# Layer 1's values by seven half-width products, sums of pixels on GpSimd, pixels read a pair of chunks at a time

## The chip, the cores and the metric

The kernel runs on one core of a Trainium2 chip. The time is that of one execution of the whole program on the device, in microseconds (us); a kernel is run several times and the median is given. One further execution is recorded by the hardware profiler, and every duration below comes from that record. The engines are called PE (TensorE matmuls), PEld (TensorE's weight loads), DVE (VectorE), ACT (ScalarE), POOL (GpSimd) and SP (SyncE, which here only issues DMAs).

## The reference

Two layers on an image tensor of 2 images, 512 channels and 64 x 64 pixels, all in fp32. Each layer normalizes its input in groups of channels and adds its result to it.

```
x = x + L0(group_norm(x))     # deformable convolution: depthwise 3x3, offsets, masks, bilinear samples
x = x + L1(group_norm(x))     # attention over all 4096 pixels of an image:

px = pixels x channels                      # 4096 x 512 for each image
q, k = tanh(px @ Wq.T), tanh(px @ Wk.T)     # 64 channels each
v = px @ Wv.T
attn = softmax(sum_p q * k * align_w)
content = (px + attn @ v) @ Wfc.T + bfc
out = relu(batch_norm(content))             # statistics over both images
```

The change is in layer 1. The kernel folds the output matrix into the values, so that it makes `v = px @ (Wv.T @ Wfc.T)` once for each image and applies it to the probabilities.

## The kernel before

Layer 0 takes up about the first 1273 us of the recorded execution. The change leaves it alone. Layer 1 then runs once for each of the two images (the loop at L1237), and its instructions stand on each engine's queue exactly in the order of the source (`tc.manual_schedule`). An engine that waits holds up everything behind it on its queue; a DMA waits on the queue of the engine that issues it.

A *chunk* is 512 pixels with all 512 channels, a tile of 128 partitions x 4 channel blocks x 512 pixels (1 MB). An image has eight chunks, taken as four *pairs* `i`. Three stages follow each other in an image.

**Values stage** (L1240 to L1261). For each pair, `pk` (L1245) computes keys and queries of both chunks on PE and `tanh` (L1249) puts them into `kq`. Then four calls of `values(i, x1, x2, t)` (L1197) each take 128 pixels of both chunks of the pair. The matmul at L1204 has pixels as the stationary operand and the folded weights `wc` (512 channels wide) as the moving one. It fills one PSUM bank for each chunk; a matmul of the program appears as two instructions in the trace. From these two banks ScalarE and VectorE make seven planes of 256 channels, the tile `v`: four blocks or differences of blocks of the values, in the form in which the later product needs them, and SP stores the tile to DRAM (`wv`, 0.9 MB). Between calls, ScalarE normalizes the chunks of the next pair (`normalize`, L1134). All chunks of an image are loaded far ahead into `xs` from the pool `cp` (eight buffers); for image 1 they are issued on ScalarE's queue. In the third pair of image 0 `output_weights` (L1215) loads the matrix `wfcT` and makes the planes `w7` from it. In the last pair `produce(0, 0)` and `produce(0, 1)` stand between the calls.

**Attention** (L1265 to L1317). For each of eight query chunks `qb` and each of 16 steps `kp`: `produce(qb, kp + 2)` computes scores (`pS`, L1172), their exponentials `e` (L1176) and four sums on VectorE; `load_values` (L1227) reads six of the seven planes of step `kp + 2` from DRAM (0.8 MB) into a ring of four buffers; six products of 256 columns go into six PSUM banks `acc` (L1309, 24 instructions). Two more steps multiply the pixels of the chunk itself (`xq`, L1288, 1 MB) by `w7`. So the product of attention and values is made of seven block products in place of eight already.

**Seventh product and finish** (L1339 to L1387). The seventh product `p7` (L1347, 72 instructions) reads the seventh planes, loaded one at a time by `load_seventh` (L1232, 0.13 MB, six buffers): six beside the last accumulation steps, ten within `p7` as buffers come free. In the last query chunk of an image these ten go into two tiles of the values ring (L1296). Within the last `p7` of image 0 the chunks and `wc` of image 1 are loaded and its first pair is normalized. Eight PSUM banks are used: `A0` to `A5` through `bank(i, ...)`, and two as one tile with the tag `st` for scores. Names ending in `_d` are in DRAM.

At the end, batch norm needs all of both images. The residuals `xr` (L1337) and the stored chunks `r` (L1403) are loaded, scaled, added and written out (L1426).

Of the kernel before, what the change touches and what calls it, by code (L numbers as in the profile page):

```python
# [9 lines left out]
F32 = mybir.dt.float32  # L10
I32 = mybir.dt.int32
AF = mybir.ActivationFunctionType
# [5 lines left out]
P = 128  # L18
NB = 2
C = 512  # L20
# [550 lines left out]
def window_path(ctx: ExitStack, tc: tile.TileContext, t_in: dict, out: bass.AP, far: bass.AP, sums: bass.AP):  # L571
# [516 lines left out]
    with ExitStack() as l1, tc.manual_schedule():  # L1088
# [8 lines left out]
        with ExitStack() as at, ExitStack() as inner:  # L1097
# [3 lines left out]
            vw = inner.enter_context(tc.tile_pool(name="w1v", bufs=3, side="right"))  # L1101
            ps = at.enter_context(tc.tile_pool(name="w1ps", bufs=1, space=PSUM))
# [25 lines left out]

            def value_output():
                t = wk.tile([P, KB, C], F32, tag="x", name="wc", bufs=1)  # L1130
                nc.sync.dma_start(t, wc_d)
                return t
# [7 lines left out]
            xs = [chunk(0, 0), chunk(0, 1)]  # L1140
            wc = value_output()
            xs += [chunk(0, ch) for ch in range(2, NCH)]
# [9 lines left out]
            normalize(xs[0], *norms[0])  # L1152
            normalize(xs[1], *norms[0])
# [43 lines left out]
            def values(i, x1, x2, t):  # L1197

                cols = slice(t * P, (t + 1) * P)
                pv = []  # L1200
                for h, x in enumerate((x1, x2)):
                    p = bank(2 * (t % 2) + h, "pv")
                    for kb in range(KB):
                        nc.tensor.matmul(p, x[:, kb, cols], wc[:, kb, :], start=(kb == 0), stop=(kb == KB - 1))  # L1204
                    pv.append(p)
                v = vw.tile([P, 7, HC], F32, name="v", bufs=4)
                nc.scalar.copy(v[:, 0, :], pv[0][:, :HC])
                nc.vector.tensor_sub(v[:, 6, :], v[:, 0, :], pv[0][:, HC:])
                nc.scalar.copy(v[:, 1:6:4, :], pv[1].rearrange("p (a c) -> p a c", a=2))
                nc.vector.tensor_add(v[:, 3, :], v[:, 5, :], pv[0][:, HC:])  # L1210
                nc.vector.tensor_sub(v[:, 2, :], v[:, 3, :], v[:, 0, :])
                nc.vector.tensor_sub(v[:, 4, :], v[:, 1, :], v[:, 2, :])
                nc.sync.dma_start(v_d[n][4 * i + t], v)

            def output_weights():  # L1215

                wfc = load_w("wfcT", C, cp, tag="c")
                wf4 = wfc.rearrange("p (h r) (i c) -> p h r i c", h=2, i=2)
                nc.scalar.copy(w7[:, :, 0, :], wf4[:, 0, :, 0, :])
                nc.scalar.copy(w7[:, :, 1, :], wf4[:, 1, :, 0, :])  # L1220
                nc.scalar.copy(w7[:, :, 5, :], wf4[:, 1, :, 1, :])
                nc.vector.tensor_sub(w7[:, :, 6, :], wf4[:, 0, :, 0, :], wf4[:, 0, :, 1, :])
                nc.vector.tensor_add(w7[:, :, 3, :], wf4[:, 0, :, 1, :], wf4[:, 1, :, 1, :])
# [3 lines left out]
            def load_values(n, kp):  # L1227
                v = vw.tile([P, 7, HC], F32, name="v", bufs=4)
                nc.sync.dma_start(v[:, :6, :], v_d[n][kp][:, :6, :])
                return v  # L1230

            def load_seventh(n, kp):  # L1232
                v = wk.tile([P, HC], F32, name="v7", bufs=6)
# [3 lines left out]
            for n in range(NB):  # L1237
                sc, bi = norms[n]
                ready = []
                for i in range(NCH // 2):  # L1240
                    for h in range(2):
                        ch = 2 * i + h
                        pk = bank(4 + h, "pk")
                        for kb in range(KB):
                            nc.tensor.matmul(  # L1245
                                pk, wkq[:, h, kb].rearrange("p h d -> p (h d)"), xs[ch][:, kb, :],
                                start=(kb == 0), stop=(kb == KB - 1),
                            )
                        nc.scalar.activation(kq[:, ch, :], pk, AF.Tanh)  # L1249
                    if i == 0:  # L1250
                        queries(0)
                    for t in range(4):
                        values(i, xs[2 * i], xs[2 * i + 1], t)
# [223 lines left out]
```

## Time and profile before

| what | us |
|---|---|
| median of three runs (3728.24 to 3731.88) | 3728.55 |
| the profiled execution, its own time | 3727.62 |
| its span, first to last instruction | 3725.8 |
| PE busy / DVE busy / ACT busy / POOL busy | 3443.0 / 2249.3 / 1290.7 / 220.5 |
| products of values, L1204, 512 instructions, PE busy | 222.4 |
| attention products, L1309, 256 columns, with `e` / with `tt` | 768.2 / 748.2 |
| seventh product, L1347, with values | 231.1 |
| values stage of image 0, first product to last | 1290.3 to 1425.1 |
| values stage of image 1, first product to last | 2468.4 to 2601.5 |

The mean granted TensorE clock over the span was 0.968 of full speed. "Busy" is the time in which at least one instruction of the kind runs; the mean length of a matmul in a group row is longer than the distance from one to the next, because matmuls are pipelined, so the pace is read from runs of them in the chain of waits.

### The profile page before, as it was taken

The numbers are of one execution on the slowest core, as the hardware profiler recorded it, in microseconds if no ns is written. First come the engines' busy times: TensorE is split into PE (matmuls) and PEld (weight loads), VectorE is DVE, ScalarE is ACT, GpSimd is POOL, SyncE is SP. The second block draws the span as 40 slices with busy tenths as digits, with TensorE's granted clock in tenths as the row PEclk, the third lists the DMA queues.
The fourth block names the chain that finished last, engine by engine and source line by source line (L and its number), as shares of the span: only waits on it lengthen the run. The fifth ranks groups of instructions, "written<-read, shape, count | busy, mean of one in ns | idle before, by whom it ended". The sixth has DMA issues, their size and how long they took to land.

```text
span 3725.8 us, 37930 instructions
## 1 busy us (share of the span) xinstructions
PE 3443.0 (92%) x14735; PEld 2359.8 (63%) x14735; DVE 2249.3 (60%) x3402; ACT 1290.7 (35%) x1659; POOL 220.5 (6%) x162
## 2 busy tenths in 40 slices
PE   4589989999998899999999999999999999999990
PEld 2255555555555446777777777764777777777770
DVE  6899989999996324545554554432455455545544
ACT  1466767777776332111111111122111121111115
POOL 2111112112111000000000000000000000000000
PEclk9789999999999899999999999999999999999995
DMA  6234432433432434334334433443433343343349
GB/s 238 62 98 128 133 123 82 126 121 94 127 96 99 163 120 162 130 109 153 128 115 138 138 131 106 157 171 120 161 120 118 108 144 113 111 135 120 124 150 394
DMA packets 179629, 499.96 MB, mean 134 GB/s; under 512 B 22096, under 2 KB 63824, under 8 KB 169968
## 3 DMA queue, kind: packets, MB, share of 16 engines
q1 hardware_dynamic: 176528, 476.48, 38.2%
q10 hardware_dynamic: 2880, 20.97, 1.4%
q8 instruction: 117, 1.92, 0.2%
q14 instruction: 72, 0.59, 0.0%
q0 software_dynamic: 32, 0.00, 0.0%
HBM read 406.09 MB, written 91.29 MB: 133 GB/s over the span
## 4 chain that ended last, share of the span: by engine, by line
PE 60%; DMA 1%; DVE 0%; ACT 0%; SPq 0%; issue 0%; ACTq 0%
PE acc L1309 41%; PE pS L1172 7%; PE p L1347 7%; PE pv L1204 4%; PE pk L1245 1%; DMA out<-ct 1%; PE pr L1273 0%; DMA v<-wv 0%; DMA r<-wx 0%; ACT ct L1421 0%; DVE r L1425 0%; SPq L1403 0%; ACT r L1421 0%; DVE ct L1425 0%; ACT e L1176 0%
## 5 line engine op out<-in xcount | busy, mean ns | idle before, releaser
L1309 PE MATMUL acc<-e,v 128*128 128x256 f32 x3072 | 768.2, 386 | 2.1 <-DMA v<-wv 2.1
L1309 PE MATMUL acc<-tt,v 128*128 128x256 f32 x3072 | 748.2, 380 | 0.0
L1176 ACT ACTIVATE e<-pS 128x1024 f32<-128x1024 f32 x256 | 262.4, 1025 | 1360.7 <-PE pS L1172 1319.1
L1309 PEld LDWEIGHTS acc<-e,v 128*128 128x128 f32 x3072 | 566.5, 190 | 235.4 <-issue 163.8
L1309 PEld LDWEIGHTS acc<-tt,v 128*128 128x128 f32 x3072 | 582.4, 190 | 90.7 <-issue 10.6
L1179 DVE TENSOR_TENSOR t<-e 128x256 f32<-128x256 f32 x256 | 108.9, 425 | 764.7 <-ACT e L1176 764.7
L786 DVE SCALAR_TENSOR_TENSOR conv<-xn,L_conv_dw_w_sb,conv 128x504 f32<-128x504 f32 (+1 forms) x512 | 400.1, 795 | 18.4 <-ACT conv L781 4.2
L1189 DVE TENSOR_TENSOR tot<-tot,e 128x512 f32<-128x512 f32 x480 | 330.2, 688 | 8.3
L947 PEld LDWEIGHTS pa<-bt,patch 96*128 96x128 f32 x2048 | 252.2, 197 | 62.9 <-issue 38.5
L1172 PE MATMUL pS<-q,kq 64*128 64x512 f32 x1024 | 289.0, 641 | 0.0
L947 PE MATMUL pa<-bt,patch 96*128 96x128 f32 x2048 | 256.2, 282 | 9.3 <-ACT dT L958 5.8
L933 ACT COPY bt<-pb 96x1024 f32<-96x1024 f32 x124 | 234.1, 2001 | 57.1 <-PE pb L928 57.1
L967 PE MATMUL py<-dT,L_conv_out_w_sb 128*128 128x512 f32 x512 | 240.0, 614 | 0.0
L756 PE MATMUL pq<-L_conv_in_w_sb,xn 128*128 128x512 f32 x512 | 236.8, 606 | 2.3 <-ACT xn L746 2.3
L1347 PE MATMUL p<-t,v 128*128 128x256 f32 x1024 | 231.1, 382 | 0.0
L1204 PE MATMUL pv<-wc,xt 128*128 128x512 f32 x512 | 222.4, 593 | 1.4 <-DVE v L1210 1.4
L1347 PEld LDWEIGHTS p<-t,v 128*128 128x128 f32 x1024 | 192.2, 190 | 46.2 <-issue 21.2
L958 ACT COPY dT<-pa 32x256 f32<-32x256 f32 x496 | 180.0, 363 | 111.4 <-PE pa L947 102.1
L840 PE MATMUL po<-om_w_pg,feat 128*128 128x432 f32 x512 | 203.5, 542 | 0.0
L967 PEld LDWEIGHTS py<-dT,L_conv_out_w_sb 128*128 128x128 f32 x512 | 100.4, 200 | 121.5 <-issue 116.7
L1204 PEld LDWEIGHTS pv<-wc,xt 128*128 128x128 f32 x512 | 96.9, 190 | 125.3 <-issue 121.7
L756 PEld LDWEIGHTS pq<-L_conv_in_w_sb,xn 128*128 128x128 f32 x512 | 94.5, 195 | 107.5 <-issue 94.1
(174 smaller groups left out, 3310.6 us busy)
## 6 DMA issues: line engine op xcount, KB each, us to landing
v<-wv SPq DMA_DIRECT2D x256, 768.0 KB
patch<-xt SPq DMA_DIRECT2D x256, 192.0 KB
v<-wv SPq DMA_DIRECT2D x256, 128.0 KB
wv<-v SPq DMA_DIRECT2D x32, 896.0 KB
xt<-xj SPq DMA_DIRECT2D x128, 128.0 KB
res<-in_x SPq DMA_DIRECT2D x64, 256.0 KB
wx<-res SPq DMA_DIRECT2D x64, 256.0 KB
xq<-wx SPq DMA_DIRECT2D x16, 1024.0 KB
```

The costliest lines, as they stand in the source:

```text
L756: nc.tensor.matmul(pq, xn[:, kb, 1 + 2 * t : 3 + 2 * t, :].rearrange("p r c -> p (r c)"), in_w[:, kb, :], start=(kb == 0), stop=(kb == KB ...
L786: nc.vector.scalar_tensor_tensor(dst, src, wt, dst, ALU.mult, ALU.add)
L840: nc.tensor.matmul(po[:, : 3 * GP], f[:, kb, t * P : (t + 1) * P], om_w[:, kb].rearrange("p a k g -> p (a k g)"), start=(kb == 0), stop=(k ...
L933: copy(bt[:SN].rearrange("s g q d -> s d (g q)")[:, d0 : d0 + 4, :], pb[:SN])
L947: nc.tensor.matmul(pa[:, p], xp[:SN, p, cb * P : (cb + 1) * P], bt[:SN, 4 * cb : 4 * cb + 4, PX * s + p, :], start=True, stop=True,)
L967: nc.tensor.matmul(py, out_w[:, kb, cb * P : (cb + 1) * P], dT[:, kb, :], start=(kb == 0), stop=(kb == KB - 1))
L1172: nc.tensor.matmul(pS[:, h, :], kq[r, 2 * (kp // 4) + h, c0 : c0 + P], qs[qb][r, :], start=True, stop=True)
L1176: nc.scalar.activation(e.rearrange("p a q -> p (a q)"), pS.rearrange("p h q -> p (h q)"), AF.Exp)
L1189: nc.vector.tensor_add(tots[qb], tots[qb], e2[:, h, :])
L1204: nc.tensor.matmul(p, x[:, kb, cols], wc[:, kb, :], start=(kb == 0), stop=(kb == KB - 1))
L1309: nc.tensor.matmul(acc[j][:, cb * HQ : (cb + 1) * HQ], v[:, j, cb * P : (cb + 1) * P], ops[j], start=(kp + cb == 0), stop=(kp + cb == NPAI ...
L1347: nc.tensor.matmul(p7[:, cb * HQ : (cb + 1) * HQ], v7[:, cb * P : (cb + 1) * P], t3, start=(k + cb == 0), stop=(k + cb == NPAIR + 2),)
```

## The change

The values of a pair of chunks are a product of matrices of 2 x 2 blocks: two chunks by two halves of the input channels, times two halves of the input channels by two halves of the output channels. The kernel before makes all eight block products. The changed one makes seven, of sums and differences of blocks (`sa`, `sb` of pixels, `wcs` of weights), each of 256 columns and two matmuls deep. Eleven VectorE operations and one ScalarE copy put the seven results together into the same seven planes. The sums of the next pair's pixels are made by GpSimd after its second chunk is normalized; those of image 0's first pair by VectorE. Sums take up buffers of `cp`, so pixels are loaded one pair ahead and not all at once. The values ring becomes a pool of its own with three buffers, the output weights are loaded at the start into two of them, the first two values loads of an image stand on ScalarE's queue after the last call, and seventh planes get 13 buffers.

```diff
+            vv = inner.enter_context(tc.tile_pool(name="w1vv", bufs=3, side="right"))
...
+            def load_pixels(n, i):
+                pair = [chunk(n, 2 * i + h) for h in range(2)]
+                return pair, [cp.tile([P, 2, 2, CH], F32, tag="c", name=name) for name in ("xsa", "xsb")]
+
+            def sum_pixels(engine, pair, sums):
+                (a1, a2), (sa, sb) = [x.rearrange("p (j r) q -> p j r q", j=2) for x in pair], sums
+                engine.tensor_add(sa[:, 0], a2[:, 0], a2[:, 1])
+                engine.tensor_sub(sa[:, 1], sa[:, 0], a1[:, 0])
+                engine.tensor_sub(sb[:, 0], a1[:, 0], a2[:, 0])
+                engine.tensor_sub(sb[:, 1], a1[:, 1], sa[:, 1])
...
+            def sum_value_output(wc):
+                t = wk.tile([P, 2, 4, HC], F32, tag="tx", name="wcs", bufs=1)
+                b = wc.rearrange("p (j r) (l c) -> p j r l c", j=2, l=2)
+                nc.vector.tensor_sub(t[:, :, 0, :], b[:, 0, :, 1, :], b[:, 0, :, 0, :])
+                nc.vector.tensor_sub(t[:, :, 1, :], b[:, 1, :, 1, :], t[:, :, 0, :])
+                nc.vector.tensor_sub(t[:, :, 2, :], b[:, 1, :, 1, :], b[:, 0, :, 1, :])
+                nc.vector.tensor_sub(t[:, :, 3, :], t[:, :, 1, :], b[:, 1, :, 0, :])
+                return t
...
-            xs = [chunk(0, 0), chunk(0, 1)]
+            pixels = {0: load_pixels(0, 0)}
             wc = value_output()
-            xs += [chunk(0, ch) for ch in range(2, NCH)]
+            pixels[1] = load_pixels(0, 1)
...
-            normalize(xs[0], *norms[0])
-            normalize(xs[1], *norms[0])
+            for x in pixels[0][0]:
+                normalize(x, *norms[0])
+            sum_pixels(nc.vector, *pixels[0])
+            wcs = sum_value_output(wc)
...
-            def values(i, x1, x2, t):
+            def values(n, i, t):
                 cols = slice(t * P, (t + 1) * P)
-                pv = []
-                for h, x in enumerate((x1, x2)):
-                    p = bank(2 * (t % 2) + h, "pv")
-                    for kb in range(KB):
-                        nc.tensor.matmul(p, x[:, kb, cols], wc[:, kb, :], start=(kb == 0), stop=(kb == KB - 1))
-                    pv.append(p)
-                v = vw.tile([P, 7, HC], F32, name="v", bufs=4)
-                nc.scalar.copy(v[:, 0, :], pv[0][:, :HC])
-                nc.vector.tensor_sub(v[:, 6, :], v[:, 0, :], pv[0][:, HC:])
-                nc.scalar.copy(v[:, 1:6:4, :], pv[1].rearrange("p (a c) -> p a c", a=2))
-                nc.vector.tensor_add(v[:, 3, :], v[:, 5, :], pv[0][:, HC:])
+                (x1, x2), (sa, sb) = pixels[i]
+                products = (
+                    (x1[:, 0:2], wc[:, 0:2, :HC]), (x1[:, 2:4], wc[:, 2:4, :HC]), (sa[:, 1], wcs[:, :, 1, :]),
+                    (sa[:, 0], wcs[:, :, 0, :]), (sb[:, 1], wc[:, 2:4, HC:]), (sb[:, 0], wcs[:, :, 2, :]),
+                    (x2[:, 2:4], wcs[:, :, 3, :]),
+                )
+                p = []
+                for j, (a, b) in enumerate(products):
+                    if j % 2 == 0:
+                        pv = bank((4 * t + j // 2) % 6, "pv")
+                    p.append(pv[:, (j % 2) * HC : (j % 2 + 1) * HC])
+                    for r in range(2):
+                        nc.tensor.matmul(p[j], a[:, r, cols], b[:, r, :], start=(r == 0), stop=(r == 1))
+                v = vv.tile([P, 7, HC], F32, name="v")
+                u = vw.tile([P, 4, HQ], F32, tag="e", name="u")
+                nc.scalar.copy(u[:, 0, :], p[0])
+                nc.vector.tensor_add(v[:, 0, :], u[:, 0, :], p[1])
+                nc.vector.tensor_add(u[:, 1, :], u[:, 0, :], p[2])
+                nc.vector.tensor_add(u[:, 2, :], u[:, 1, :], p[3])
+                nc.vector.tensor_add(u[:, 3, :], u[:, 2, :], p[4])
+                nc.vector.tensor_add(v[:, 5, :], u[:, 2, :], p[5])
+                nc.vector.tensor_add(u[:, 1, :], u[:, 1, :], p[5])
+                nc.vector.tensor_sub(v[:, 1, :], u[:, 1, :], p[6])
+                nc.vector.tensor_add(v[:, 3, :], u[:, 3, :], v[:, 5, :])
                 nc.vector.tensor_sub(v[:, 2, :], v[:, 3, :], v[:, 0, :])
+                nc.vector.tensor_sub(v[:, 6, :], v[:, 0, :], u[:, 3, :])
                 nc.vector.tensor_sub(v[:, 4, :], v[:, 1, :], v[:, 2, :])
                 nc.sync.dma_start(v_d[n][4 * i + t], v)
...
-            def load_values(n, kp):
-                v = vw.tile([P, 7, HC], F32, name="v", bufs=4)
-                nc.sync.dma_start(v[:, :6, :], v_d[n][kp][:, :6, :])
+            def load_values(n, kp, queue=nc.sync):
+                v = vv.tile([P, 7, HC], F32, name="v")
+                queue.dma_start(v[:, :6, :], v_d[n][kp][:, :6, :])
                 return v
             def load_seventh(n, kp):
-                v = wk.tile([P, HC], F32, name="v7", bufs=6)
+                v = wk.tile([P, HC], F32, name="v7", bufs=13)
...
+                for j in range(2 if n == 0 else 0):
+                    wf.append(vv.tile([P, 7, HC], F32, name="v")[:, :4, :].rearrange("p (r i) c -> p r i c", r=2))
+                    nc.sync.dma_start(
...
                 for i in range(NCH // 2):
+                    if 0 < i < 3 or n and i == 0:
+                        k = i + 1 if i else 1
+                        pixels[k] = load_pixels(n, k)
+                    pk = ps.tile([P, 2, CH], F32, tag="st", name="pk")
...
                     for t in range(4):
-                        values(i, xs[2 * i], xs[2 * i + 1], t)
-                        if n == 0 and i == 2 and t == 0:
-                            output_weights()
+                        values(n, i, t)
+                        if wf and i == 0 and t == 0:
+                            output_weights(wf)
                         if t in (0, 1) and i + 1 < NCH // 2:
-                            normalize(xs[2 * i + 2 + t], sc, bi)
+                            normalize(pixels[i + 1][0][t], sc, bi)
+                            if t:
+                                sum_pixels(nc.gpsimd, *pixels[i + 1])
                         if i + 1 == NCH // 2 and t in (1, 2):
                             produce(0, t - 1)
-                        if i + 1 == NCH // 2 and t > 1:
-                            ready.append(load_values(n, t - 2))
+                ready = [load_values(n, kp, nc.scalar) for kp in range(2)]
...
-                        if NPAIR - 6 <= kp < NPAIR:
-                            v7s[kp - NPAIR + 6] = load_seventh(n, kp - NPAIR + 6)
-                        if qb + 1 == NCH and kp in (NPAIR - 2, NPAIR - 1):
-                            vg = vw.tile([P, 7, HC], F32, name="v", bufs=4)
...
+                        if 3 <= kp < NPAIR:
+                            v7s[kp - 3] = load_seventh(n, kp - 3)
...
-                        if 0 <= kp and kp + 6 < NPAIR and qb + 1 < NCH:
-                            v7s[kp + 6] = load_seventh(n, kp + 6)
+                        if 0 <= kp < 3:
+                            v7s[kp + 13] = load_seventh(n, kp + 13)
...
                         if qb + 1 == NCH and n + 1 < NB:
-                            if 0 <= kp < 6:
-                                xs[kp] = chunk(n + 1, kp)
-                            if kp == 6:
+                            if kp == 0:
+                                pixels[0] = load_pixels(n + 1, 0)
                                 wc = value_output()
-                            if kp in (7, 10):
-                                normalize(xs[kp // 9], *norms[n + 1])
+                            if kp == 4:
+                                wcs = sum_value_output(wc)
+                            if kp in (6, 8):
+                                normalize(pixels[0][0][kp // 2 - 3], *norms[n + 1])
+                            if kp == 8:
+                                sum_pixels(nc.gpsimd, *pixels[0])
...
-                if n + 1 < NB:
-                    xs[6:] = [chunk(n + 1, ch) for ch in (6, 7)]
```

## The prediction

> **What bounds the kernel now.** I read the page's engine rows and chain first, to see which engine the span hangs on; then the stretch of layer 1 in which the values are made, in the chain of waits in order of time and in the table by stage; then the groups, for durations; last the end of the kernel, where another resource might hold the gain.
>
> ```profile
> PE 3443.0 (92%) x14735; PEld 2359.8 (63%) x14735; DVE 2249.3 (60%) x3402; ACT 1290.7 (35%) x1659; POOL 220.5 (6%) x162
> ...
> PE 60%; DMA 1%; DVE 0%; ACT 0%; SPq 0%; issue 0%; ACTq 0%
> ```
>
> Sixty per cent of the chain is TensorE in layer 1, and nothing else has more than one per cent beside it. Now the values stage.
>
> ```profile
> 1302.00:1324.00 22.00, 22.00 (x53) 9.77 (x52) 4.66 (x11) 5.93 (x10) 0.00 (x0) 1.00 0.32 131
> ...
> 3625.00:3635.00 10.00, 10.00 (x48) 8.81 (x47) 0.55 (x1) 0.00 (x0) 0.00 (x0) 1.00 1.01 423
> ```
>
> In the table by stage (stretch, length, busy PE, PEld, DVE, ACT, POOL, granted clock, DMA share, GB/s) PE is busy for all of 22 us at clock 1.00, DVE for 4.66, POOL not at all, DMA at 0.32. So in the values stage an instruction taken from PE is time taken from the kernel, and DVE and POOL have room. The second row is the end of the kernel: from about 3625 the DMA engines are full and stay so. That stage starts when PE has finished the last accumulation, so it moves with PE and neither swallows nor adds to the gain, except for bytes added to it.
>
> ```profile
> 1388.25 6.87 PE pk L1245 x16
> 1395.12 13.73 PE pv L1204 x32
> ...
> 1427.57 6.02 DMA v<-wv
> ...
> 1522.35 15.54 PE acc L1309 x72
> ...
> 2502.85 27.47 PE pv L1204 x64
> ```
>
> The chain in order of time (start, length, what) gives the pace: 64 instructions of 512 columns in 27.47 us, 0.4293 each; 72 of 256 columns in 15.54 us, 0.2158 each, half of that. The 6.02 is a values load that PE waits for when attention starts.
>
> ```profile
> L1309 PEld LDWEIGHTS acc<-e,v 128*128 128x128 f32 x3072 | 566.5, 190 | 235.4 <-issue 163.8
> ...
> L1204 PE MATMUL pv<-wc,xt 128*128 128x512 f32 x512 | 222.4, 593 | 1.4 <-DVE v L1210 1.4
> ...
> L810 POOL TENSOR_TENSOR sq<-feat 128x512 f32<-128x512 f32 x16 | 20.4, 1275 | 97.6 <-ACT feat L807 97.6
> ...
> L1212 DVE TENSOR_TENSOR v<-v 128x256 f32<-128x256 f32 x32 | 13.6, 425 | 1.1
> ```
>
> These groups (busy us, mean ns of one, idle before) give durations: a weight load, the old product with the 1.4 us it waited, a GpSimd and a VectorE operation. Two rows of the view by tile add what the two engines do to each other in layer 0 (shortest, median, longest ns):
>
> ```profile
> L786 DVE SCALAR_TENSOR_TENSOR conv<-xn,L_conv_dw_w_sb,conv x512: 643/744/1746, 48.2 to 1118.0; 128x504 f32<-128x504 f32 x128, 128x512 f32<-128x512 f32 x43
> ...
> L794 POOL TENSOR_TENSOR tot<-tot,conv x32: 1263/1608/1651, 72.4 to 1118.9; 128x512 f32<-128x512 f32 x32
> ```
>
> **The change part by part.** One profiled execution took 3727.62 us (span 3725.8); the median of the runs is 3728.55, 0.93 more.
>
> *Seven products.* A call of values issues 2 x 4 matmuls of 512 columns, 16 instructions, since every matmul appears as two: 16 x 0.4293 = 6.87 us. The new one issues 7 x 2 of 256 columns, 28 instructions: 28 x 0.2158 = 6.04. Over 32 calls 219.8 becomes 193.4: -26.4 us. Weight loads grow from 512 to 896. The row: acc has one 190 ns load for each 216 ns matmul and still runs at 0.2158 a pair, so the loads are hidden. The Trainium skill (TensorE: Matmul & The Clock Gate, Part 3, The mechanism) says that a load overlaps running matmuls only where the row group differs; all loads here use all 128 rows. By that rule 384 more loads would add 384 x 0.190 = 73 us, and the change would lose 47. The row rules it out for this very form; I take -26.4.
>
> *VectorE.* Per call four operations become eleven, and ScalarE keeps one copy of two. At 425 ns and 0.46 us from start to start (dependent ones start at 1411.02, 1411.48 and 1411.94 in the timeline) eleven take 5.1 us, below PE's 6.04. A pair of chunks is 6.87 + 4 x 6.04 = 31.0 us of PE against 20.2 of DVE: 10.8 us of cover. PSUM is now a ring of six banks of which a call uses four, so PE may run one and a half calls ahead. Cost 0. Without cover it would be the excess of DVE over PE.
>
> *Sums of pixels on GpSimd.* Four operations of 1024 elements, for three pairs of each image and for image 1's first pair. Nearest row: 1.27 us for 512 elements, so up to 2.5; half of the 4.5 us that the Trainium skill states for 2048 (GPSIMD Engine Reference, 3.1) is 2.25. I take 2.4: 9.6 us, begun about 18 us into a pair (pk 6.87, a call 6.04, two products 1.7, a copy and a normalization 3.5) and needed at 31.0 + 6.87 + 1.7 = 39.6. By themselves hidden; POOL has nothing else to do here. But the rows show L786 going from 744 to 1746 ns and L794 from 1263 to 1651: the two engines get in each other's way. The skill's rule (SBUF — State Buffer, Who interferes with whom) is harsher than an average shows: an operation with two SBUF inputs on DVE and a reading one on GpSimd exclude each other for a whole instruction. The last four of the eleven have both inputs in SBUF; the other seven read PSUM. Alternating strictly, those four lose up to 4 x 2.4 = 9.6 us. Followed through: GpSimd starts during the second call, VectorE ends the third 8 to 10 us after PE, the fourth (5.1 against PE's 6.04) 7 to 9 us after, and the next pair's first bank is read some 3 us before PE wants it, because pk gives 6.87 us in between. By the row's average (1 us lost per GpSimd operation) the cost is 0, by the rule 0 to 1.4 us a pair. I take 0.5 in all; bounds 0 (a lock gives nothing back) and 6 x 4 = 24.
>
> *First pair.* Its sums and the weight sums are on VectorE: 4 x 1.22 (1024 elements, between 688 ns for 512, L1189, and 2291 for 2048, L1330) + 4 x 0.69 = 7.6 us from 1285.1, where the second chunk is normalized. pk ends at 1290.3; the third product comes at 1292.0 and needs what is ready at 1291.5. Cost 0, bounds 0 and +3. For image 1 the weight sums wait on VectorE for wc, issued at 2445.3 as before, so until about 2452; behind them stand bn_stats and, at 2461.7, the multiply of finish_chunk, which is soon enough. GpSimd's first sums have from about 2456 to 2470 there. Hidden.
>
> *Pixels a pair ahead.* In image 0 the loads stand on SP's queue behind the last store of the pair before, which waits for VectorE's lag: issued some 9 us into the pair. At the start of layer 1 the first of two megabyte loads was used 6.3 us after issue (1273.06 to 1279.39); with the store ahead of them 7 to 9. ScalarE's normalization waits for them, and behind it the copies of later calls, which PE needs only after 1.5 calls. Cost 0.5, bounds 0 and +8. Before, PE never waited for pixels, so nothing is gained. In image 1 they stand on ScalarE's queue ahead of tanh, which waits for pk anyway, and start at once.
>
> *Output weights.* Loaded at the start and not at the third pair: the 1.4 us of PE idle at L1204 goes. The two loads stand on SP ahead of the first store, due 10 us later; six megabytes in all at 420 GB/s land by about 1291. The three copies (0.6 each) and four VectorE operations (2.8) now stand between the first and second calls, within the one and a half calls of room. -1.4, bounds -1.4 and +2.
>
> *Start of attention.* The first two values loads move to ScalarE's queue and wait for the stores of the second and third last calls, with ring buffers cut from four to three; exp of step 2 stands behind them. A store lands in under 5 us, so the loads arrive in time; but step 0 begins with bank 3, which the last call holds until VectorE has read it. VectorE also has produce's six operations (3.1 us) ahead of that call's eleven and ends 4.5 us after PE; its read of bank 3 is the seventh, four short operations earlier: 2.6 us after PE's end, where PE wants it at 1.06. About 1.5 us of wait per image in place of the 1.0 (from 1432.6 to 1433.6) of before: +0.5 each, +1.0; bounds -2 and +8.
>
> *Ring of three within attention.* A load can now start when the step before has ended, 2 x 6.44 + 1.06 = 13.9 us before use; it takes 6.0. Cost 0.
>
> *Seventh planes.* Thirteen buffers: thirteen loads lie beside accumulation steps and three, not ten, in the p7 products. In the last query chunk those three (0.39 MB) fall into the full DMA stretch: 0.39 / 0.423 = +0.9. The two late residual loads no longer wait for PE, but the DMA engines were full: 0.
>
> Sum: -26.4 - 1.4 + 0.5 + 0.5 + 1.0 + 0.9 = -24.9. The 1.8 us around the span stay. 3727.62 - 24.9 = 3702.7; with the 0.93 of the median 3703.7, rounded 3704.
>
> **The rivals.** *GpSimd and VectorE block each other* or pixels come late, so PE waits at banks. For: the L786 maximum and the lock rule. Against: 10.8 us of cover a pair. Price 1.4 to 4 us in each of six pairs, 8 to 24 in all: 3712 to 3728.
>
> *The products don't run at the pace of acc*, because PE follows VectorE's 5.1 us plus waits call by call: no saving. Against: VectorE's sum is below PE's. Some 3728.
>
> *Slower: the ring of three values buffers.* Place: steps 2 to 4 of each query chunk, where xq (1 MB), the store of ct (image 0) and values loads share the DMA engines. It decides once a load takes over 13.9 us. At 1 us late in three steps of 16 chunks it costs 48 us: 3752. It eats the gain from 1.6 us a chunk on. Against: 2.8 MB at 400 GB/s are 7 us.
>
> **How the numbers follow.** Forecast 0.75 (3699 to 3709). A little better, if all waits are nil: 0.06 (3697 to 3700). Blocking: 0.12, two thirds of it still faster. No saving: 0.03. Ring: 0.04. Faster by over 0.2% (7.5 us, what a measurement of this kernel can tell from no change): 0.75 + 0.06 + 0.08 = 0.89; same 0.04 + 0.03 = 0.07; slower 0.04. The range 3697 to 3716 takes in the first two and the milder half of the third.
>
> **What would show it.** Right: runs of 28 pv instructions in about 6.04 us; acc unchanged with idle near 2 to 3 us; xsa and xsb on POOL near 2.4 us; some of the last four VectorE operations of a call stretched by about 2 us; the 1.4 us at the copies gone. Wrong: idle at pv behind VectorE of more than a microsecond a pair, idle at acc behind values loads beyond the first steps, or pv instructions at 0.25 us.

## The result and the profile after

The changed kernel takes 3708.14 us (median of five runs, 3706.09 to 3709.22), against 3728.55 before (five runs, 3726.36 to 3731.88): a ratio of 0.9944, 95% interval 0.993 to 0.9959. The gain is 20.4 us where 24.9 was forecast. One profiled execution took 3706.09 us with a span of 3704.3, so 21.5 us less than the one of before; the rest of the difference is that the five runs lie higher above it (2.05 us in place of 0.93).

The page of the changed kernel, its engine row and its chain:

```profile
PE 3418.5 (92%) x15119; PEld 2432.2 (66%) x15119; DVE 2383.6 (64%) x3638; ACT 1271.1 (34%) x1627; POOL 289.2 (8%) x190
...
PE 75%; DVE 16%; DMA 5%; ACT 1%; issue 1%; SPq 1%; POOL 1%; ACTq 0%; DVEq 0%; POOLq 0%
```

PE has 24.5 us less to do with 384 more instructions. DVE and DMA now have shares in the chain. More than half of DVE's 16% is layer 0 (conv, L786, alone has 9%), which did not change: the chain is followed back through waits, and a new wait in layer 1 leads it through other work in layer 0. So I read layer 1 by stretches. First the table by stage (stretch, length, busy PE, PEld, DVE, ACT, POOL, granted clock, DMA share, GB/s), one pair of chunks in image 0, one in image 1, and ten microseconds of the end:

```profile
1315.35:1347.80 32.45, 31.31 (x129) 24.24 (x129) 24.44 (x45) 8.31 (x14) 9.75 (x4) 1.00 0.46 179
...
2482.52:2513.88 31.36, 31.31 (x130) 24.24 (x129) 23.32 (x45) 8.22 (x14) 9.77 (x4) 1.00 0.51 185
3634.30:3644.30 10.00, 0.00 (x0) 0.00 (x0) 7.89 (x5) 10.00 (x15) 0.00 (x0) 0.50 1.05 399
```

The groups (busy us, mean ns of one, idle before) and the chain have the new products and the sums:

```profile
L1238 PE MATMUL pv<-wc,xsb 128*128 128x256 f32 x128 | 33.5, 384 | 2.7 <-DVE v L1242 2.5
L1252 DVE TENSOR_TENSOR v<-v 128x256 f32<-128x256 f32 x32 | 24.1, 754 | 0.0
L1138 POOL TENSOR_TENSOR xsa<-xt 128x1024 f32<-128x1024 f32 x7 | 16.5, 2358 | 1287.4 <-ACT xt L1160 1287.4
```

```profile
1387.07 12.09 PE pv L1238 x56
```

56 instructions, two calls, in 12.09 us are 0.216 each, as forecast, and a GpSimd sum takes 2.36 us, as forecast; but PE waits for VectorE, and L1252 has a mean of 754 ns where 425 were assumed. A pair took 34.34 us before; by the prediction it takes 31.0. In image 0 it takes 32.45, with PE idle for more than a microsecond. PEld is busy for 24.24 of it and DVE for 24.44, not 20.2, and POOL for 9.75. The end is full of DMA as before. The rows of PE, DVE and POOL in order of time in that pair (start, length, engine, line) say where it idles:

```profile
1344.94 1.13 PE L1238 MATMUL pv<-wc,xsb 128*128 128x256 f32 x4 [1.14 <-DVE v L1242]
```

```profile
1334.66 0.42 DVE L1248 TENSOR_TENSOR v<-u,pv 128x256 f32<-128x256 f32 x1
1335.00 2.07 DVE L1249 TENSOR_TENSOR v<-u,v 128x256 f32<-128x256 f32 x1
1337.11 2.46 DVE L1250 TENSOR_TENSOR v<-v 128x256 f32<-128x256 f32 x1
1339.49 2.57 DVE L1251 TENSOR_TENSOR v<-v,u 128x256 f32<-128x256 f32 x1
1341.98 2.57 DVE L1252 TENSOR_TENSOR v<-v 128x256 f32<-128x256 f32 x1
1344.47 0.41 DVE L1242 TENSOR_TENSOR v<-u,pv 128x256 f32<-128x256 f32 x1
```

```profile
1334.44 2.36 POOL L1138 TENSOR_TENSOR xsa<-xt 128x1024 f32<-128x1024 f32 x1 [22.95 <-ACT xt L1160]
1336.87 2.42 POOL L1139 TENSOR_TENSOR xsa<-xsa,xt 128x1024 f32<-128x1024 f32 x1
1339.25 2.53 POOL L1140 TENSOR_TENSOR xsb<-xt 128x1024 f32<-128x1024 f32 x1
1341.74 2.53 POOL L1141 TENSOR_TENSOR xsb<-xt,xsa 128x1024 f32<-128x1024 f32 x1
```

The four VectorE operations with both inputs in SBUF (L1249 to L1252, the second call's) each last as long as one GpSimd sum; L1248, which reads PSUM, takes 0.42 us in the middle of a GpSimd sum. So do all seven such operations of the second call in the first pair (1301.77 to 1304.68), beside sums that run from 1301.70 on. The third call's first operation starts at 1344.47 and not at 1336.5, where its copy is ready, and the fourth call's third bank, which is the third call's first, waits for it.

Layer 0 does not repeat exactly: in the recorded executions its end (the first product of the group norm after it) lies anywhere from 1273.5 to 1282.3 us with the same code up to there. So that differences of a few microseconds are not lost in this, I compare the starts of rows in the trace from that product on. It gives 2450.44 us to the end before and 2428.11 after, 22.33 less, of which a layer 0 that was 0.83 longer took some back. Stretch by stretch (us):

| stretch | before | after | change |
|---|---|---|---|
| group norm to the first pk | 4.95 | 4.89 | -0.06 |
| first pk to the first product of values | 9.99 | 8.44 | -1.55 |
| image 0, four calls of the first pair | 27.46 | 25.66 | -1.80 |
| second pair / third pair, pk to pk | 34.34 / 35.99 | 32.45 / 32.41 | -1.89 / -3.58 |
| fourth pk to the first accumulation | 38.00 | 34.87 | -3.13 |
| first to second accumulation step | 7.54 | 6.41 | -1.13 |
| all query chunks up to the last p7 | 1012.3 | 1012.3 | 0 |
| last p7 of image 0 | 15.54 | 15.69 | +0.15 |
| image 1, first / second / third pair, pk to pk | 34.33 / 34.33 / 34.34 | 33.04 / 31.36 / 31.34 | -1.29 / -2.97 / -3.00 |
| fourth pk to the first accumulation | 37.99 | 35.10 | -2.89 |
| first to second accumulation step | 7.53 | 6.41 | -1.12 |
| issue of the residual loads to the end | 107.35 | 109.29 | +1.94 |

### The profile page after: what moved, and what is told of

It is laid out like the page before. It is cut to its first block, busy times and chain, and to the rows that moved or that the text cites. A ratio compares the mean times of both kernels' runs of the same rounds, so it can differ in the third digit from the quotient of the medians.

```text
span 3704.3 us, 38937 instructions
## 1 busy us (share of the span) xinstructions
PE 3418.5 (92%) x15119; PEld 2432.2 (66%) x15119; DVE 2383.6 (64%) x3638; ACT 1271.1 (34%) x1627; POOL 289.2 (8%) x190
## 4 chain that ended last, share of the span: by engine, by line
PE 75%; DVE 16%; DMA 5%; ACT 1%; issue 1%; SPq 1%; POOL 1%; ACTq 0%; DVEq 0%; POOLq 0%
PE acc L1351 41%; DVE conv L786 9%; PE pS L1198 7%; PE p L1389 6%; PE pq L756 5%; PE py L967 4%; PE pa L947 4%; PE pv L1238 3%; PE pk L1292 1%; PE p_mean L799 1%; DMA patch<-xt 1%; DMA out<-ct 1%; DVE pk L883 1%; DVE o L845 1%; SPq L912 1%
## 5 line engine op out<-in xcount | busy, mean ns | idle before, releaser
L1202 ACT ACTIVATE e<-pS 128x1024 f32<-128x1024 f32 x256 | 262.0, 1024 | 1386.7 <-PE pS L1198 1313.2
L786 DVE SCALAR_TENSOR_TENSOR conv<-xn,L_conv_dw_w_sb,conv 128x504 f32<-128x504 f32 (+1 forms) x512 | 400.1, 795 | 18.3 <-ACT conv L781 4.1
L840 PEld LDWEIGHTS po<-om_w_pg,feat 128*128 128x128 f32 x512 | 93.0, 191 | 90.3 <-issue 89.4
L1198 PEld LDWEIGHTS pS<-q,kq 64*128 64x128 f32 x1024 | 77.1, 184 | 84.9 <-issue 84.9
```

Of the source, the lines that this page charges most:

```text
L786: nc.vector.scalar_tensor_tensor(dst, src, wt, dst, ALU.mult, ALU.add)
L840: nc.tensor.matmul(po[:, : 3 * GP], f[:, kb, t * P : (t + 1) * P], om_w[:, kb].rearrange("p a k g -> p (a k g)"), start=(kb == 0), stop=(k ...
L1198: nc.tensor.matmul(pS[:, h, :], kq[r, 2 * (kp // 4) + h, c0 : c0 + P], qs[qb][r, :], start=True, stop=True)
L1202: nc.scalar.activation(e.rearrange("p a q -> p (a q)"), pS.rearrange("p h q -> p (h q)"), AF.Exp)
```

## The experiments

Each edit is against the changed kernel. The median is of five executions, in e7_four_banks of twelve. The columns after the ratio come from one trace each: from the group norm to the end, the first pk of image 0 and the four calls behind it, pairs two and three of image 0, the first pair of image 1, from the fourth pk of each image to its first accumulation, and from the issue of the residual loads to the end. The first pk has the same instructions in all of these kernels and takes 8.4 or about 10 us all the same; the 1.6 us between belong to no edit.

| kernel | median us | ratio to before, interval | to the end | first pk, four calls | pairs 2, 3 | image 1, pair 1 | to acc, image 0 / 1 | residuals to end |
|---|---|---|---|---|---|---|---|---|
| changed kernel | 3708.14 | 0.9944 (0.993 to 0.9959) | 2428.11 | 8.44, 25.66 | 32.45, 32.41 | 33.04 | 34.87 / 35.10 | 109.29 |
| e1_vector | 3704.2 | 0.9933 (0.9919 to 0.9946) | 2423.32 | 8.36, 25.20 | 31.04, 31.04 | 31.72 | 34.86 / 34.85 | 108.37 |
| e2_halves | 3700.55 | 0.9922 (0.9908 to 0.9936) | 2423.27 | 10.01, 24.17 | 31.04, 31.04 | 31.04 | 35.00 / 35.26 | 108.97 |
| e3_queue | 3707.75 | 0.9938 (0.9924 to 0.9951) | 2426.68 | 9.94, 24.72 | 31.36, 31.36 | 32.84 | 34.88 / 34.83 | 109.27 |
| e4_seventh | 3705.7 | 0.9933 (0.9919 to 0.9946) | 2426.08 | 10.01, 24.73 | 32.53, 32.27 | 31.36 | 35.02 / 35.11 | 108.34 |
| e5_banks | 3707.36 | 0.9943 (0.993 to 0.9957) | 2428.01 | 8.40, 25.71 | 32.53, 32.73 | 32.31 | 34.91 / 34.73 | 108.97 |
| e7_four_banks | 3739.44 | 1.0026 (1.0017 to 1.0034) | 2453.11 | 10.02, 28.15 | 36.48, 34.78 | 36.49 | 35.14 / 34.83 | 109.06 |
| e6_combined | 3701.53 | 0.9926 (0.9913 to 0.994) | 2421.78 | 9.79, 24.17 | 31.04, 31.04 | 31.04 | 34.94 / 34.85 | 108.49 |
| e8_first_load | 3699.22 | 0.9923 (0.9909 to 0.9937) | 2421.82 | 9.72, 24.17 | 31.04, 31.04 | 31.04 | 34.71 / 34.71 | 108.68 |
| e9_old_order | 3699.4 | 0.9923 (0.9909 to 0.9937) | 2421.24 | 10.02, 24.17 | 31.04, 31.04 | 31.04 | 34.70 / 34.70 | 108.38 |

**e1_vector: no sums on GpSimd.**

```
- sum_pixels(nc.gpsimd, *pixels[i + 1])      # and the same for pixels[0] of image 1
+ sum_pixels(nc.vector, *pixels[i + 1])
```

> All sums of pixels on VectorE in place of GpSimd. Theory (lock): a GpSimd sum and a VectorE operation with two SBUF inputs exclude each other, and this is what stretches four VectorE operations of each third call from 0.42 to 2.0-2.6 us; TensorE's waits for banks behind them are 1.4 + 1.4 us in image 0, 0.6 + 0.3 + 0.3 in image 1 and up to 1.4 at image 1's first call, 5.4 us in all. On VectorE the sums take 4 x 1.22 = 4.9 us a pair, less than the 7 to 8 us that the stretching costs, so the stretched operations go back to 0.42 us, the waits inside the pairs go to 0, that at image 1's first call to about 0.5: some 4.5 us faster than the changed kernel, 3703 to 3704.5. Rival (VectorE is merely too full: eleven operations a call, no lock): 4.9 us more work on VectorE in each pair makes TensorE wait longer, 3708 or slower.

Measured: 4.79 us less from the group norm to the end, pairs of 31.04. The pairs give 5.2 us; in this trace PE also waits 1.3 us for a seventh plane in the last p7 of image 0, and the end is 0.9 shorter. VectorE's rows in the second pair:

```profile
1333.49 0.42 DVE L1249 TENSOR_TENSOR v<-u,v 128x256 f32<-128x256 f32 x1
1333.94 0.42 DVE L1250 TENSOR_TENSOR v<-v 128x256 f32<-128x256 f32 x1
1334.28 0.42 DVE L1251 TENSOR_TENSOR v<-v,u 128x256 f32<-128x256 f32 x1
1334.62 0.42 DVE L1252 TENSOR_TENSOR v<-v 128x256 f32<-128x256 f32 x1
1334.95 1.22 DVE L1138 TENSOR_TENSOR xsa<-xt 128x1024 f32<-128x1024 f32 x1
```

Without GpSimd beside them the same four take 0.42 us, and the sums 1.22 each in place of 2.4 to 2.5. VectorE does more in each pair and PE waits less: the trouble was not VectorE's load but the blocking.

**e2_halves: the same GpSimd work in shorter operations.**

```
- engine.tensor_add(sa[:, 0], a2[:, 0], a2[:, 1])              # and the other three likewise
+ for r in (0, 1) if engine is nc.gpsimd else (slice(0, 2),):
+     engine.tensor_add(sa[:, 0, r], a2[:, 0, r], a2[:, 1, r])
```

> The sums stay on GpSimd, each of the four cut into two of 512 elements (eight of about 1.27 us). Lock theory: a VectorE operation waits for one GpSimd operation, so each of the last four of a call loses at most 1.3 us and not 2.5; the third call's loss halves to 4 or 5 us and the rest falls on the next call's last four. TensorE's waits in the pairs (1.4 + 1.4 + 0.6 + 0.3 + 0.3 = 4.0 us) go to nearly 0, that at image 1's first call stays or shrinks: about 3704. Rival (the two engines share a port by time, a loss in proportion to GpSimd's busy time): the same total busy time, so the same loss, 3708.

Measured: 4.84 us less although the first pk took 1.57 more; none of the pairs has a wait left, and those that are timed from pk to pk are at 31.04, image 1's first included. VectorE's rows in the second pair:

```profile
1332.43 0.69 DVE L1250 TENSOR_TENSOR v<-u,v 128x256 f32<-128x256 f32 x1
1333.15 1.38 DVE L1251 TENSOR_TENSOR v<-v 128x256 f32<-128x256 f32 x1
1334.45 1.49 DVE L1252 TENSOR_TENSOR v<-v,u 128x256 f32<-128x256 f32 x1
1335.86 1.49 DVE L1253 TENSOR_TENSOR v<-v 128x256 f32<-128x256 f32 x1
...
1340.09 1.25 DVE L1250 TENSOR_TENSOR v<-u,v 128x256 f32<-128x256 f32 x1
1341.37 1.37 DVE L1251 TENSOR_TENSOR v<-v 128x256 f32<-128x256 f32 x1
1342.67 0.41 DVE L1252 TENSOR_TENSOR v<-v,u 128x256 f32<-128x256 f32 x1
```

(Lines are one higher here.) GpSimd is busy no less than before (10.7 against 9.8 us a pair), but an operation of VectorE waits for one of GpSimd's, now half as long: the second call loses 3.4 us in place of 8.0, the third the 1.8 that are left. A loss in proportion to busy time, the rival, is out: VectorE loses 5.2 us in place of 8.0 beside more GpSimd work. What counts is how long a single GpSimd operation is and how many of VectorE's two-input operations meet one.

**e3_queue: image 0's pixels early.**

```
- (nc.scalar if n else nc.sync).dma_start(t, x1_d[n][ch])
+ (nc.scalar if n or ch > 3 else nc.sync).dma_start(t, x1_d[n][ch])
```

> Image 0's pixels of the third and fourth pair are loaded from ScalarE's queue ahead of tanh, as image 1's are, and not from SP's behind a store. Theory (late pixels move the sums to a worse time): in image 0 the sums begin 19.0 us into a pair, in image 1 17.9; that puts a whole GpSimd operation of 2.4 us in place of 1 us in front of VectorE's first two-SBUF operation, and TensorE loses 1.4 us a pair in place of 0.3. With the loads early, image 0's two pairs come to 31.35 us like image 1's: 2.2 us faster than the changed kernel, 3706, and ScalarE no longer waits for xt. Rival (the pixels' queue doesn't matter, the stretching in image 0 has another cause, the weights say): pairs of 32.4 us as before, 3708.

Measured: the two pairs come down by 1.09 and 1.05 us to 31.36, what image 1 had; L1249 in the second pair lasts 0.98 us in place of 2.07. The time to the end fell by 1.43 only, since the first pk took 9.94 us and not 8.44. The pixels' lateness never made PE wait for pixels; it moved the sums by about 1 us, so that a whole one stood in front of VectorE.

**e4_seventh: the last seventh planes ahead of the residual loads.**

```
- v = wk.tile([P, HC], F32, name="v7", bufs=13)
+ v = wk.tile([P, HC], F32, name="v7", bufs=14)               # planes 14 and 15: two free buffers of t3
...
+ if final and NPAIR - 3 <= kp < NPAIR: v7s[kp] = load_seventh(n, kp, final)    # final: last query chunk of image 1
...
- if 0 <= kp < 3:
+ if 0 <= kp < 3 and not final:
```

> In the last query chunk the last three seventh planes are loaded during the last three accumulation steps (into a fourteenth buffer and two free ones of t3), ahead of the residual loads. Theory (wait): the last of these loads, issued at 3603.4 among 8 MB of residual loads, lands 12.2 us later, TensorE waits 1.9 us for it before its last two products, and everything behind moves with it: from the end of the last accumulation to the span's end 103.3 us as in the kernel before, not 105.25, 3706.2 in all. Rival 1 (bytes, the prediction's term): 0.39 MB leave the stretch in which the DMA engines are full: -0.9. Rival 2 (the full DMA engines hold the end, and the wait is covered): no change.

The wait was this, in the chain of the changed kernel:

```profile
3603.40 12.19 DMA v<-wv
3615.59 0.04 issue
3615.63 1.15 PE p L1389 x4
```

PE idles 1.91 us there. The wait is gone in e4_seventh, and yet from the issue of the residual loads to the end 108.34 us are left, 0.95 less and not 1.9. The six kernels that load these planes late take 108.99 us in the mean here (108.37 to 109.29), the four that load them ahead 108.47 (108.34 to 108.68). So most of the wait was hidden, in a stretch in which the DMA engines are full. What early loading gives, 0.5 to 1.0, fits the 0.9 that the bytes were priced at, but that it is the bytes is not shown: these are single traces, and e1_vector, which loads late, took 108.37, no longer than the early ones. Even the early ones take a microsecond more than the kernel before (107.35), for as many bytes (42.1 MB), at 389 and not 392 GB/s; why, these runs don't tell.

The edit gained a second time, where nothing was expected: image 1's first pair took 31.36 us in place of 33.04. With a fourteenth buffer the load of `wc` no longer stands behind a seventh plane that waits for its buffer; it was issued 0.6 us before p7 began (2439.86 against 2440.49) and not 3.2 us into it (2436.84 against 2433.63), and VectorE had summed the weights (0.69 us each) before GpSimd began. In the changed kernel the two met, and finish_chunk's multiply, for which PE's first bank waits 1.37 us, stood behind:

```profile
2447.10 2.14 DVE L1152 TENSOR_TENSOR wcs<-wc 128x512 f32<-128x512 f32 x1 [10.26 <-DMA wc<-wvfc]
2449.28 2.72 DVE L1153 TENSOR_TENSOR wcs<-wc,wcs 128x512 f32<-128x512 f32 x1
2451.92 2.83 DVE L1154 TENSOR_TENSOR wcs<-wc 128x512 f32<-128x512 f32 x1
...
2456.47 1.20 DVE L1414 TENSOR_TENSOR t<-p,rin 128x1024 f32<-128x1024 f32 x1
```

**e5_banks: the free banks first.**

```
- for j in (3, 4, 5, 2, 1, 0) if kp == 0 ...
+ for j in (4, 5, 0, 1, 2, 3) if kp == 0 ...
```

> Only the order of the six accumulators in the first attention step of a chunk is changed: banks 4, 5, 0, 1, 2, 3, so that the two banks which the last call of values doesn't use come first and bank 3, which it uses last, comes last. Theory: TensorE's wait at the start of attention is the wait for VectorE's read of bank 3; it measured 0.5 us in image 0 and, with 0.33 of it for a values load, 0.7 in image 1. From the fourth pk to the first accumulation 34.87 and 35.10 us become 34.4 and 34.7, 0.9 us in all. By the prediction's own figure (VectorE reads bank 3 2.6 us after TensorE's end, wanted at 1.06) it would be 1.5 an image, 3.0 in all. Rival: the wait is for the values load alone, no change.

Measured: 34.91 in image 0 (34.87 before the edit) and 34.73 in image 1 (35.10). Image 1's 0.4 is what was expected, but e1_vector and e3_queue came down as far (34.85 and 34.83) with the old order, and image 0 did not move. So the theory of bank 3 gets no support; that the load is the cause was left to the last two runs.

**e7_four_banks: without the two spare banks.**

```
- pv = bank((4 * t + j // 2) % 6, "pv")
+ pv = bank((4 * t + j // 2) % 4, "pv")
```

> The products of values go through a ring of four PSUM banks in place of six, nothing else is changed (the sums stay whole, on GpSimd). Theory: the two more banks are what covers VectorE while it is held up: the fourth call's first product then waits for VectorE's first operation of the third call and not its fifth product for it. In image 0 it is wanted at 1340.2 and released at 1344.9: 4.7 us of wait in place of 1.1; in image 1 3.6 in place of 0.3; about 3.5 us more in each of six pairs, some 21 us in all: 3729, the gain is gone. Rival (the cover comes from VectorE's free time at the next pk, banks don't matter): 3708.

Measured: 25.0 us more from the group norm to the end (expected 21), of which 1.6 are a slower first pk, pairs of 34.8 to 37.5, and the whole gain gone. PE's waits in image 0's values stage and the start of attention (total, times, longest):

```profile
PE pv L1238 <- DVE v L1242: 10.7, 3, 3.7
```

In the changed kernel that line reads 2.5 us, 1.1 at most. So the ring of six banks carried most of the blocking, and the waits that were left are what it could not carry. The profiled execution (3729.93) is the shortest of the twelve; what the others spend up to 14 us more on is not recorded.

**e6_combined, e8_first_load, e9_old_order: together.** The first is e2, e4 (in the last query chunk of both images) and e5 in one. The second adds this, and the third is the second with the old order of banks:

```
+ if i + 1 == NCH // 2 and t == 2:
+     ready.append(load_values(n, 0, nc.scalar))
- ready = [load_values(n, kp, nc.scalar) for kp in range(2)]
+ ready.append(load_values(n, 1, nc.scalar))
```

> Three edits together: the GpSimd sums in halves, the last three seventh planes of the last query chunk of both images loaded ahead (14 buffers, and two free ones of t3), and the accumulators' order that begins with the two free banks. From the first product of the group norm to the end the changed kernel took 2428.1 us, with the halves 2423.3. Expected: all pairs of chunks at 31.04 us (no wait in the values stage), no wait for seventh planes at either last chunk (0.15 to 1.56 us at image 0's), 0.9 us less at the two starts of attention, and at the end 0.95 less if bytes are what counts there, 1.9 if the wait does: 2420.5 to 2422, some 7 us under the changed kernel. Rival (the waits give way to others, or the end is fixed by the DMA engines): 2423 as the halves alone.

> The three edits of e6_combined and, beside them, the first values load of attention issued one call earlier on ScalarE's queue (ahead of exp, no longer behind the last call's copy). Theory: what is left of the wait at the start of attention (34.94 and 34.85 us from the fourth pk to the first accumulation in e6_combined, 35.00 and 35.26 in e2_halves) is that load; it lands 5.4 us after its issue, and issued some 7 us earlier it is there in time: 34.7 in both images, 0.4 us in all, 2421.4 from the first product of the group norm to the end. Rival (VectorE's last reads of the last call hold it): 34.9 as before. If the load delays the call's store or the copies behind it, it is slower than e6_combined.

> The same with the accumulators in the changed kernel's order, bank 3 first. Theory (the load alone sets the start): 34.7 us from the fourth pk to the first accumulation in both images, as in e8_first_load. The prediction's step (VectorE reads bank 3 too late): about 0.5 or more above e8_first_load at each image's start.

Measured: e6_combined 6.33 us under the changed kernel to the end, inside its range, with a first pk that took 1.35 more. With the first load issued earlier both orders start attention after 34.7 us in both images. So the 0.2 and 0.4 us that the changed kernel lost here (34.87 and 35.10) were the first values load, whose issue on ScalarE's queue stood behind the last call's copy, and bank 3 costs nothing. The landings in the traces agree: in the changed kernel the load is complete at 1414.77 and 2580.03, and the first accumulation begins at 1414.91 and 2580.16; in e9_old_order it is complete more than 6 us ahead. The time to the end of e8_first_load does not show its 0.4 us (2421.82 against 2421.78): its first pk started 0.2 later and its end took 0.2 longer. e9_old_order, 6.87 us under the changed kernel, has no wait of PE left in the values stage. Its table by stage, a pair of each image:

```profile
1344.09:1375.13 31.04, 31.04 (x130) 24.32 (x129) 20.74 (x46) 8.33 (x14) 10.57 (x8) 1.00 0.50 193
2506.21:2537.25 31.04, 31.04 (x130) 24.32 (x129) 20.32 (x45) 8.22 (x14) 10.57 (x8) 1.00 0.42 163
```

Against the kernel before it is 0.9923 (0.9909 to 0.9937); that it also beats the changed kernel is read from the traces, since the two intervals against the kernel before overlap.

## Why the prediction was right, and where its terms were off

- *Seven products, -26.4: shown.* Where nothing waits a pair takes 31.04 us in place of 34.34 in every kernel that removes the blocking: 8 x 3.30 = 26.4. All 896 loads (190 ns each) stay hidden, as the row of acc said, and against the rule of the Trainium skill (TensorE: Matmul & The Clock Gate, Part 3, The mechanism).
- *VectorE's eleven operations, 0: shown*, by e1_vector, where VectorE has 4.9 us more in pairs two and three and PE doesn't wait inside them, and *the ring as cover: shown* by e7_four_banks.
- *Sums on GpSimd, +0.5: the step that failed.* Against 31.04 a pair and 24.17 for the first four calls, image 0 lost 1.50, 1.41 and 1.37 us and image 1 2.00, 0.32 and 0.30: 6.9. Of this, 1.0 is the weight sums of image 0's first pair on VectorE, a term of its own (*First pair*, put at 0): e1_vector, without any sum on GpSimd, loses 1.03 there. The other 5.9 are blocking, image 1's start (PE idle for 1.37, called "soon enough") among it. The length of a sum (2.4), the lag of the third call (8.0) and the form of the blocking were as worked out, the rule's and not the row's average. What went wrong is where the lag was held against PE: at the next pair's first bank, which has the 6.87 us of pk ahead of it. The bank that runs out first is the fourth call's third, one and a half calls, 9.1 us, behind. The figure given for the rule, 0 to 1.4 us a pair, is what image 0 shows (1.41 and 1.37), but since the lag was followed to the next pair's bank and not to this one, that is luck.
- *Pixels a pair ahead, +0.5: under-sized.* e3_queue gives 2.1 us for two pairs, as more blocking and not as a wait for pixels; they are part of the 5.9.
- *Output weights, -1.4: -1.65*, by the third pair (35.99 against 34.34 before; no such excess after).
- *Start of attention, +1.0: wrong in sign, -1.7.* The second step's wait for its load (1.03 and 1.02) went, and 0.2 to 0.4 came in its place, not for bank 3 but for the first load. VectorE's read of bank 3 (L1248, ended 1414.54) came 0.8 us after PE's last product (1413.76), not 2.6, because produce's six operations were over at 1411.6, while PE still worked on the last call; and PE had scores to make until 1414.8.
- *Seventh planes, +0.9: compatible, but not shown.* The end took 1.94 more, of which e4_seventh takes back 0.95, though a wait of 1.9 went; the other microsecond stays open.
- *Ring of three, 0: shown*: all query chunks take 1012.3 us as before.
- *Not foreseen:* the first pk took 8.44 us in place of 9.99 (-1.55). It is no part of the change: of the eleven traces only those of the changed kernel, e1_vector and e5_banks show 8.4, the others 9.7 to 10.0. Nor is it a clear gain: in these three, and in no other, PE then waits 0.7 to 0.8 us for the weight sums. That is the 1.0 above; where the first pk is slow, the weight sums cost nothing, as forecast.

The wait for the weight sums, in the changed kernel's trace:

```profile
1292.08 1.99 PE L1238 MATMUL pv<-wcs,xsa 128*128 128x256 f32 x8 [0.67 <-DVE wcs L1153]
```

Added up: -26.4 + 5.9 (blocking) + 1.0 (weight sums) - 1.65 - 1.7 + 1.9 + 0.15 (last p7 of image 0) - 1.6 (up to the first product of values) = -22.4 from the group norm on, for a measured 22.33.

The rival "GpSimd and VectorE block each other" (0.12) did happen, a little under the low end of its price (5.9 against 8 to 24). One of the signs that the prediction had named for being wrong is there too: PE idles at pv behind VectorE for 1.14 and 1.10 us in image 0's second and third pair. The gain in the profile is 3.4 us short of the forecast: the blocking took 4.9 more than its two terms (0.5 each), the first pair's weight sums 1.0 and the end 1.2 more; the start of attention gave 2.7 more, and output weights, the first pk and layer 0 together 1.0. So the seven products were foreseen for the right reason, and that the sum of the rest came this near is in part luck: the start of attention, which had the wrong sign, made up for about half of the blocking.

## What to carry to other kernels

GpSimd is no free hand beside VectorE: count which of VectorE's operations have two inputs in SBUF, take for each that meets GpSimd the length of one GpSimd operation, and hold the lag against every buffer of the ring, not only against the next stage. If the work must be on GpSimd, cut it into short operations; if VectorE has the time, it does the sum in half the time and blocks nobody. Where the spread of an unchanged part is as large as the effect, compare stretches between the same two instructions of each trace.

## What the runs showed of the hardware that was not expected

The blocking is one for one. A sum of 1024 elements on GpSimd takes 2.35 us alone and up to 2.53 where it alternates with 0.42 us operations of VectorE, and each of these takes up to 2.57. With sums of 512 elements it is 1.27 alone for the sum and up to 1.49 for the VectorE operation. Beside the same sums VectorE's operations with one input in PSUM keep their 0.42 us (seven from 1337.27 on in e2_halves). This agrees with the Trainium skill (SBUF — State Buffer, Who interferes with whom), which names two SBUF inputs on VectorE against a GpSimd instruction that reads SBUF, and calls the ports that they share an exclusive lock. It holds for `scalar_tensor_tensor` too (`finish_chunk` in e4_seventh: two took 3.69 us in place of 1.42).

The granted clock at the start of layer 1 is not the same from run to run. PE is all but idle there for about 8 us, and in both traces its clock stands at 0.50 when the first pk begins. In the two microseconds from 1284 on it stood at 0.97 in the changed kernel's trace and still at 0.50 in the trace of before, which reached 0.89 in the next two (two rows of the tables by stage, before and after):

```profile
1284.00:1286.00 2.00, 2.00 (x4) 0.86 (x3) 0.00 (x0) 1.14 (x2) 0.00 (x0) 0.50 1.03 434
...
1284.00:1286.00 2.00, 2.00 (x5) 0.87 (x5) 0.06 (x1) 1.91 (x3) 0.00 (x0) 0.97 1.04 438
```

Before, the first pk began at 1280.31 and ran at half clock for about 5.9 us; after, it began at 1281.08 and did so for about 3.0. Half of the difference is 1.5 us, which is what the first pk differs by. What decides when the clock comes back, these traces do not tell.
